# A four-layer graph kernel: layer 3's masks on GpSimd, hop 2's counts a step later, first rows by SyncE's queue

## The chip, the cores and the metric

The kernel runs on one core of one Trainium2 chip. The metric is the device time of one execution in microseconds (us), as the median of several runs. A profiled execution gives the trace from which all durations below come. Engines carry the profile's names: PE is TensorE (PEld its weight loads), DVE is VectorE, ACT is ScalarE, POOL is GpSimd, SP is SyncE; SPq is SyncE's queue of transfers.

## What is computed

The input is x (3327 nodes, 64 features) and a weighted adjacency matrix adj (3327 x 3327). Four layers follow one another, each a residual step with a layer norm: `x = layernorm(x + layer(x))`. Layer 0 and layer 1 (a hyperbolic attention over all pairs of nodes) are not touched here. Layers 2 and 3 are:

```
# layer 2
for k in range(2):                       # hop 1, hop 2
    agg = adj @ x
    x = tanh(concatenate([agg, x], axis=1) @ W[k])

# layer 3
support = input @ weight
mask = (adj != 0)
rank = cumsum(mask, axis=1)
deg = rank[:, -1:]
k = minimum(deg, 100)
pos = rank - (deg - k)
w = mask * where(pos > 0, 0.5 ** (k - pos), 0)
out = w @ support + bias
```

Layer 3 needs, for each entry of adj that is not zero, the number of such entries that follow it in its row; the weight is a power of one half of that number.

## The kernel before

The adjacency matrix lies transposed in HBM, padded to 3328 x 3328 floats: 26 blocks jb of 128 rows (`adjT[jb]`, 1.70 MB each). A block is a tile of 128 partitions x 3328 elements; its two halves h of 1664 columns are worked on apart, and a half holds four chunks of 416 columns. Seven blocks stay in SBUF through layer 2 (`kept`: blocks 19 to 25); the others are loaded anew for each hop.

**Order of work.** From layer 1 on, TensorE's, ScalarE's, VectorE's and GpSimd's instructions stand in the order in which the program writes them (`manual_schedule`). Each engine, and SyncE's queue of transfers, works its own list in that order and waits for semaphores; a buffer that is written anew waits for its last reader.

**Hop 2 of layer 2** (the loop at L585, k = 1) goes through `order`: five blocks still in SBUF from hop 1 (`ready`, so r = 5), then four pairs of a new block and a kept block of the `soon` list (25, 24, 23, 22), then the other new blocks; the last three kept blocks (`end`) come in `chunk_end`. For each block `add` (L514) issues 16 products with `hw`, four for each chunk; a new block is loaded (L216) into one of five buffers, which comes free when the products and the mask of its last block are through.

Beside these products, hop 2 makes masks (1 where adj is not zero, in bf16) and counts them, for layer 3 needs the totals by block before it begins:

- `t_masks` (L444) makes the two half masks of a streamed block into scratch tiles `t_at`; in hop 2 these are the two halves of `tm`.
- `both_masks` (L353) makes the mask of a whole block that is to stay for layer 3. It goes to `over` or to a half of a kept block's tile that hop 2 has used up (`slots_of`); `place` says at which step which block goes where.
- `t_counts` (L451) issues eight products with `upto` for each mask made, which add up the totals by block in PSUM (`t_ps`).

In hop 2 the counts come at once after the masks when both halves of `tm` are made, or when more than four half masks are waiting. When all 26 blocks are counted, `t_out` (L461, L463) writes the totals to HBM (`t_rows`), and `rows_of` (L431) puts each resident block's row of totals into row 0 of its mask, both by GpSimd's queue.

**Layer 3** has 52 steps (h, jb), 26 for each half of the columns; nine blocks' masks are resident, so 34 half masks have to be made anew. `load` (L345) brings a half block into one of four `ah` buffers by SyncE's queue. `masks` (L366) makes its mask on VectorE into one of six buffers of `l3m`, then issues on SyncE's queue the transfer of row 0 (L368) and the next `load`. One of the six buffers is at first `m0`, the first row's entries.

For a step q, `count` (L644) multiplies the mask with a triangular matrix into PSUM bank c (c = 0, 1: two chunks each), `read` turns a bank into weights by a maximum with zero (on VectorE, L657, or on ScalarE, L659), and `products` (L861, and L878 for the low part, gathered over seven steps) multiplies the weights with the features. There is one PSUM tile for each bank, so the next count of a bank waits for its read. In the loop (L1031) step q does, in this order: read bank 0 (ScalarE), read bank 1 (VectorE at odd q, ScalarE at even q), one piece of the list `with_step`, at most one `masks`, and then for each bank the products of step q - 3 and the count of step q + 1.

Before the loop stands the layer's beginning: the last chunks of hop 2 (`chunk_end`), the layer norm of layer 2 (`finish`, `squares`, `sums`, `roots`, `factor`, in four parts A, B, C, E of the blocks) and the splitting of the features into bf16 parts (`first_part`, `rest_of`, `other_parts`). `roots` (L750 to L760) is nine small VectorE operations one after another. What is left of the parts C and E is in `with_step`, and so is `firsts_weighted` (L478 to L480 on VectorE: the weights of the first row of each block, after which `m0` is given back), in the fourth place, and `first_rows` (L893, L897: 16 small transfers by GpSimd's queue of the first rows' features to `sf`), in the seventh. `first_products` (L904) uses both, at step 25 of the loop and once more in the second half.

Of the kernel before, what the change touches and what calls it, by code (L numbers as in the profile page):

```python
# [15 lines left out]
ALU = mybir.AluOpType  # L16
# [5 lines left out]
NB = 26  # L22
NP = NB * P
D = 64
CW = 416
HALF = NP // 2
NBH = NB // 2
# [7 lines left out]
CPH = HALF // CW  # L35
# [10 lines left out]
BATCH_T = 2  # L46
MASKS = 6
# [34 lines left out]
def kernel(  # L82
# [11 lines left out]
    nc = tc.nc  # L94
# [218 lines left out]
    def layers(ctx, x2, x3, begun_here, kept, ready, ahead_ctx, strm):  # L313
# [9 lines left out]
        over = carry.tile([P, NP], BF16, name="over")  # L323
# [12 lines left out]
        mask, ws = {}, {}  # L336

        ahead, to_load = {}, []

        def load():  # L340
            if to_load:
                q = to_load.pop(0)
                h, jb = steps[q]
                ahead[q] = l3w.tile([P, HALF], F32, tag="ah", bufs=LOADS, name=f"ah_{h}_{jb}")
                nc.sync.dma_start(  # L345
                    ahead[q], adjT[jb * P : (jb + 1) * P, h * HALF : (h + 1) * HALF]
                )
# [3 lines left out]
        def both_masks(jb, at):  # L351

            nc.vector.tensor_scalar(at, blocks[jb], 0.0, None, ALU.not_equal)  # L353
            resident[jb] = at
            if jb not in t_done:
                t_done.add(jb)
                t_made.extend((jb, h, m) for h, m in enumerate(halves_of(at)))

        def slots_of(jb):
            at = kept[jb].bitcast(BF16)  # L360
            return at[:, :NP], at[:, NP:]

        def masks(q):
            h, jb = steps[q]
            mask[q] = l3m.tile([P, HALF], BF16, tag="mask", name=f"mask_{h}_{jb}")
            nc.vector.tensor_scalar(mask[q], ahead.pop(q), 0.0, None, ALU.not_equal)  # L366
            half = slice(h * HALF, (h + 1) * HALF)
            nc.sync.dma_start(mask[q][:1, :], t_rows[jb + 1 : jb + 2, half])  # L368
            load()
# [63 lines left out]
        def halves_of(t):  # L433
            return [t[:, h * HALF : (h + 1) * HALF] for h in range(2)]
# [12 lines left out]
        def t_counts():  # L447
            while t_made:
                jb, h, m = t_made.pop(0)
                for c in range(CPH):  # L450
                    nc.tensor.matmul(  # L451
                        t_ps[h][c * 32 : (c + 1) * 32, :], upto[:, 31 - jb : 63 - jb],
                        m[:, c * CW : (c + 1) * CW], start=(h, c) not in t_begun,
                        stop=len(t_done) == NB, skip_group_check=True,
                    )
                    t_begun.add((h, c))
# [25 lines left out]
        with tc.tile_pool(  # L482
# [6 lines left out]
            for k in range(2):  # L489
# [37 lines left out]
                if k:  # L527
                    end = [jb for jb in kept if jb not in soon]
                    r = len(order)
                    for jb in soon:  # L530
                        order += [others.pop(0), jb]
                    order += others
                    place = {
                        1: [(soon[0], over)],
                        r + 1: list(zip(soon[1:3], slots_of(soon[0]))),
                        r + 3: list(zip((soon[3], end[0]), slots_of(soon[1]))),
                        r + 7: list(zip(end[1:], slots_of(soon[3]))),
                    }
                    for i, at in zip((-2, -1), slots_of(soon[2])):
                        place[len(order) + i] = [(order[i], at)]  # L540
                    t_at = halves_of(tm)
                else:
                    stay = list(kept)
                    stay, end = stay[:-2], stay[-2:]
                    share = -(-len(others) // len(stay))
                    for i, jb in enumerate(stay):
                        order += [jb] + others[i * share : (i + 1) * share]
# [38 lines left out]
                for i, jb in enumerate(order):  # L586
                    if jb not in blocks:
                        if len(seen) % (UNDER_WAY + MORE) < MORE :
                            blocks[jb] = held[jb] = block(more, jb, tag="bt", name=f"bt_l2_{k}_{jb}")
                        else:  # L590
                            blocks[jb] = block(strm, jb, tag="at", name=f"at_l2_{k}_{jb}")
                        seen[jb] = blocks[jb]
                    if i or not k:
                        for c in range(CPH):
                            add(c, jb)
                    if k and len(t_made) > 2 * BATCH_T:
                        t_counts()
                    if jb not in t_done and jb not in kept and (k or i >= FIRST_T):
                        t_masks(jb)
                        if len(t_made) >= len(t_at):  # L600
                            t_counts()
                    if k:
                        for b, at in place.get(i, ()):
                            both_masks(b, at)
                    if k == 0 and begun_here:

                        if i == 8:
                            for c in range(CPH):
                                bottom(c)

                            warm_t = small.tile([P, 1], F32, tag="warm", name="warm_t")
                            nc.scalar.activation(warm_t, hT[:, :1], AF.Tanh)
                    if k and len(t_done) == NB and not t_ends:
                        t_ends.append(i)
                        t_counts()
                        t_out()
                        rows_of(resident)
                if k:
# [89 lines left out]
        nc.gpsimd.memset(sf, 0.0)  # L708
        for _ in range(LOADS):
            load()  # L710
        y_all, e_all, p_all = (l3n.tile([P, NB], F32, name=f"root_{k}") for k in "yep")
        parts = ((10, 3), (7, 3), (4, 3), (0, 4))
        A, B, C, E = range(4)
# [62 lines left out]
        def x3_later(i):  # L776
            scaled(i, halves(x3[:, slots(i)]), x3)
# [4 lines left out]
        def first_part(i):  # L782
            nc.scalar.copy(s12[:, slots(i), 0, :], rr[:, slots(i)])

        def rest_of(i):
            sl = slots(i)
            nc.vector.tensor_tensor(rr[:, sl], rr[:, sl], s12[:, sl, 0, :], ALU.subtract)  # L787

        def other_parts(i):
            sl = slots(i)  # L790
            nc.scalar.copy(s12[:, sl, 1, :], rr[:, sl])
            nc.gpsimd.tensor_tensor(s3[:, sl], rr[:, sl], s12[:, sl, 1, :], ALU.subtract)
# [92 lines left out]

        def first_rows():

            with nc.allow_non_contiguous_dma(reason="one row of each block"):
                for cg in range(CPH):
                    e = cg % 2  # L890
                    for h in range(2):
                        at = slice(cg * 32 + h * NBH, cg * 32 + (h + 1) * NBH)
                        nc.gpsimd.dma_start(  # L893
                            sf[at, 0, :],
                            s12[:1, h::2].rearrange("p n t d -> p n (t d)"),
                        )
                        nc.gpsimd.dma_start(sf[at, 1, e * D : (e + 1) * D], s3[:1, h::2])  # L897

        def first_products(h):

# [116 lines left out]
        def firsts_weighted():  # L1017
            nonlocal m0
            first_weights(m0)
            m0 = None  # L1020
# [1 line left out]
        first_out = None  # L1022
        with_step = [
            lambda: other_parts(B), lambda: first_part(C), lambda: rest_of(C),
            lambda: (other_parts(C), firsts_weighted()), lambda: first_part(E), lambda: rest_of(E),
            lambda: (other_parts(E), first_rows()), lambda: x3_later(C), lambda: x3_later(E),
        ]
        products(0, 0)
        advance(1, 2)
        products(0, 1)  # L1030
        for q in range(LEAD, len(steps) + LEAD + 1):  # L1031
            turn = q == NB + LEAD
            read(0, q, False)
            if turn:
                first_out = half_out(0, sums_out(0))
            read(1, q, q % 2 == 1)
            if with_step:
                with_step.pop(0)()
            while consumed and consumed[0] <= q:
                consumed.pop(0)  # L1040
            if to_mask and len(consumed) - len(to_mask) + (m0 is not None) < MASKS:
                masks(to_mask.pop(0))
            p = q - LEAD if q < NB + LEAD else q - LEAD - 1
            for c in range(2):
                if p and not turn:
                    products(p, c)
                if q < len(steps):
                    advance(c, q)
                if turn:
                    next(first_out)  # L1050
            if first_out is not None and not turn:
                next(first_out, None)
# [994 lines left out]
```

## Time and profile before

| what | value |
|---|---|
| runs | 552.70, 553.89, 554.96 us; median 553.89 |
| profiled execution | 552.03 us, of which its span 550.2 |
| busy share | PE 93%, DVE 71%, ACT 53%, POOL 42% |
| layer 3's masks (L366, DVE) | 34, each about 1.02 us |
| hop 2 of layer 2 | about 320 to 405 us |
| beginning of layer 3 | about 405 to 427 us |
| loop of layer 3 | about 427 to 537 us |

A page of the profile has six parts. The first gives busy times by engine, the second 40 equal slices of the span, in tenths; the slices from the 24th on are hop 2 and layer 3:

```profile
PE   8889999999999999999999999888998789989992
DVE  6899999999999999799444231637137986666314
POOL 4599999999999998000000000000260280000000
DMA  8978766666766545799998019957963799975001
```

GpSimd is idle from the 17th slice on but for the transfers and the few small operations at the beginning of layer 3. The fourth part follows the chain that ended last back from the end:

```profile
DMA ah<-in_adjT 4%; PE cnt L644 4%; PE cnt L514 3%; PE acc L861 3%; PE acc L878 3%; DVE w L657 2%; DMA at_l<-in_adjT 2%; DVE mask L366 1%; PE both L732 1%; ACT w L659 1%; PE cnt L923 0%; DVE sq L765 0%; DVE tm L444 0%; DVE l_var L744 0%; DVE sq L787 0%
```

In a timeline a line gives the start and the length in us, the engine, the line of the program, the operation, what it writes and reads with their sizes, and in brackets the idle time of the engine before it with what ended it.

### The profile page before, as it was taken

What the parts mean: (1) busy time and instruction counts of PE and PEld (TensorE: products, weight loads), DVE (VectorE), ACT (ScalarE), POOL (GpSimd) and SP (SyncE); (2) the same over time, 40 slices, a digit from 0 to 9 for tenths busy, and PEclk for the clock granted to TensorE, in tenths of its full rate; (3) what the DMA queues carried; (4) which work ended last, traced back from release to release, by engine and by line L of the source; (5) the groups of instructions that cost most, each with busy time, mean ns of one, the idle gap of its engine ahead of it and who ended that gap; (6) DMA issues with size and microseconds to landing.
All of it is one profiled execution on the core that took longest, in us unless ns stands there. A gap on an engine that the chain in (4) does not pass through costs nothing. (4 is left out here: it accounts for less than half of the span.)

```text
span 550.2 us, 7634 instructions
## 1 busy us (share of the span) xinstructions
PE 509.8 (93%) x2865; PEld 210.8 (38%) x2865; DVE 390.7 (71%) x563; ACT 293.3 (53%) x345; POOL 232.6 (42%) x121
## 2 busy tenths in 40 slices
PE   8889999999999999999999999888998789989992
PEld 5522222222222222854433354333444344454542
DVE  6899999999999999799444231637137986666314
ACT  4899999999999997610000000000016755566641
POOL 4599999999999998000000000000260280000000
PEclk9999999999999999899999999989999999999996
DMA  8978766666766545799998019957963799975001
GB/s 287 366 227 293 244 222 224 240 215 220 238 215 233 184 147 226 299 418 427 424 424 368 0 31 408 412 186 269 414 209 102 259 372 395 404 291 188 0 1 37
DMA packets 34137, 139.20 MB, mean 253 GB/s; under 512 B 11199, under 2 KB 12977, under 8 KB 28971
## 3 DMA queue, kind: packets, MB, share of 16 engines
q1 hardware_dynamic: 30571, 137.40, 67.3%
q0 software_dynamic: 1184, 0.63, 0.5%
q10 hardware_dynamic: 2336, 0.59, 0.5%
q8 instruction: 24, 0.39, 0.3%
q14 instruction: 22, 0.18, 0.1%
HBM read 136.93 MB, written 1.04 MB: 251 GB/s over the span
## 5 line engine op out<-in xcount | busy, mean ns | idle before, releaser
L1260 POOL TENSOR_TENSOR sg<-sg,at 128x1664 f32<-128x1664 f32 x44 | 163.6, 3738 | 1.3 <-ACT sg L1248 1.2
L1288 ACT ACTIVATE pq<-pq,al,ga 128x832 f32<-128x832 f32 x104 | 104.7, 1011 | 10.8 <-DVE a L1287 10.5
L1275 PE MATMUL pq<-riT,ljT 64*128 64x416 f32 x416 | 100.8, 561 | 10.4 <-DVE v L1296 6.2
L1296 DVE SCALAR_TENSOR_TENSOR v<-pq,a 128x832 f32<-128x832 f32 x104 | 105.8, 1018 | 3.2 <-ACT pq L1288 2.2
L1287 DVE SCALAR_TENSOR_TENSOR a<-pq,sg 128x832 f32<-128x832 f32 x104 | 105.7, 1016 | 0.5 <-PE prep_fours L1366 0.4
L1305 PE MATMUL acc<-v,xv 128*64 128x416 f32 x416 | 95.3, 537 | 0.0
L514 PE MATMUL cnt<-at_l,lj 128*64 128x416 f32 x496 | 90.1, 514 | 0.1
L1248 ACT ACTIVATE sg<-lb,rb 128x1664 f32<-128x1664 f32 (+1 forms) x53 | 87.2, 1649 | 0.0
L623 ACT ACTIVATE x<-cnt 128x416 f32<-128x416 f32 x8 | 4.1, 517 | 151.2 <-PE cnt L514 151.2
L659 ACT ACTIVATE w<-cnt 128x832 int16<-128x832 f32 x79 | 65.6, 864 | 34.9 <-PE cnt L644 34.4
L463 POOL DMA_DIRECT2D t_rows<-tb x4 | 2.6, 711 | 148.7 <-DVE tb L461 148.6
L1275 PEld LDWEIGHTS pq<-riT,ljT 64*128 64x128 f32 x416 | 31.3, 184 | 83.7 <-DVE v L1296 82.9
L514 PEld LDWEIGHTS cnt<-at_l,lj 128*64 128x64 f32 x496 | 34.9, 137 | 50.6 <-issue 49.3
L861 PE MATMUL acc<-w,s 128*128 128x416 bf16 x208 | 52.5, 339 | 1.3 <-DVE sq L765 0.5
L1305 PEld LDWEIGHTS acc<-v,xv 128*64 128x64 f32 x416 | 20.6, 134 | 61.8 <-issue 58.0
L657 DVE TENSOR_SCALAR w<-cnt 128x832 int16<-128x832 f32 x25 | 25.5, 1022 | 25.6 <-PE cnt L644 25.6
L514 PE MATMUL cnt<-kept,lj 128*64 128x416 f32 x224 | 43.4, 533 | 0.0
L366 DVE TENSOR_SCALAR mask<-ah 128x1664 bf16<-128x1664 f32 x34 | 35.5, 1058 | 7.0 <-DMA ah<-in_adjT 5.1
L644 PE MATMUL cnt<-mask,tri 128*128 128x416 bf16 x136 | 34.8, 338 | 6.0 <-DVE w L657 3.5
L444 DVE TENSOR_SCALAR tm<-at_l 128x1664 bf16<-128x1664 f32 x20 | 19.5, 1022 | 21.1 <-PE t L451 21.1
L644 PEld LDWEIGHTS <-tri 128*128 128x128 bf16 x208 | 19.5, 97 | 34.4 <-issue 17.7
L1260 POOL TENSOR_TENSOR sg<-sg,kept 128x1664 f32<-128x1664 f32 (+1 forms) x10 | 30.0, 3017 | 0.0
(316 smaller groups left out, 455.5 us busy)
## 6 DMA issues: line engine op xcount, KB each, us to landing
at_l<-in_adjT SPq DMA_DIRECT2D x27, 1664.0 KB, 11.7
at<-in_adjT SPq DMA_DIRECT2D x44, 832.0 KB, 4.8
ah<-in_adjT SPq DMA_DIRECT2D x34, 832.0 KB, 6.4
kept<-in_adjT SPq DMA_DIRECT2D x7, 1664.0 KB
bt_l<-in_adjT SPq DMA_DIRECT2D x6, 1664.0 KB
lb<-lf_rows SPq DMA_DIRECT2D x2, 384.0 KB, 5.7
mask<-t_rows SPq DMA_DIRECT2D x34, 3.2 KB
ljT<-ljT SPq DMA_DIRECT2D x4, 128.0 KB, 3.9
```

The lines of the kernel that those rows point to most:

```text
L366: nc.vector.tensor_scalar(mask[q], ahead.pop(q), 0.0, None, ALU.not_equal)
L514: nc.tensor.matmul(acc[c][h * D : (h + 1) * D, :], hw[:, slot(jb), :], blocks[jb][:, o : o + CW], start=c not in begun, stop=last, skip_gr ...
L644: nc.tensor.matmul(cnt[c][:, e, :], tri, mask[q][:, of], start=True, stop=True, skip_group_check=True,)
L659: nc.scalar.activation(w.bitcast(I16), cnt[c], AF.Relu)
L861: nc.tensor.matmul(acc[h, c][:, e, :], s12[:, slot(jb)].rearrange("p t d -> p (t d)"), ws[q, c][:, e, :], start=first, stop=last,)
L1248: nc.scalar.activation(sg[:, :, of], lbs[:, :, of], AF.Sigmoid, bias=rb[:, sl : sl + 1])
L1260: nc.gpsimd.tensor_tensor(sg[:, :, of], sg[:, :, of], at[:, :, of], ALU.mult)
L1275: nc.tensor.matmul(pq[:, h, :], ljT[h != jb // NBH][rows, of], riT[rows, ch * CW : (ch + 1) * CW], start=True, stop=True,)
L1287: stt(a_s[t], pqs[t], CUBIC_PLUS, us.pop(t), op0=ALU.add, op1=ALU.mult)
L1288: nc.scalar.activation(pqs[t], pqs[t], AF.Square, bias=al[:, one], scale=ga[:, one])
L1296: stt(w, pqs.pop(t), CUBIC_REST, a_s.pop(t), op0=ALU.add, op1=ALU.mult)
L1305: nc.tensor.matmul(accs[cp, ci][h * D : (h + 1) * D, :], xv[:, slot(jb), :], w[:, h, :], start=(jb == orders[cp][0]), stop=(jb == orders[c ...
```

## The change

Four things are done.

1. In hop 2, `place` puts at most one kept mask at a step, and later: the masks stand at steps 1, r+2, r+4, r+5, r+8, r+9 and r+12. From step r+1 on the scratch masks have a second place: the halves of block 25's first slot, in turn with `tm`. `t_counts` is called at each step, after the step's products and before its masks, so masks are counted a step after they were made.
2. `masks` runs on GpSimd, as two comparisons: equal to zero, then less than one half. The first five are issued before the layer's beginning, right after the first loads. Bank 1 is read by VectorE at every step.
3. `firsts_weighted` moves to the tenth place of `with_step` (step 12 of the loop, before step 6).
4. `first_rows` goes to SyncE's queue, two transfers at each of the eight steps 13 to 20.

```diff
         def masks(q):
             h, jb = steps[q]
             mask[q] = l3m.tile([P, HALF], BF16, tag="mask", name=f"mask_{h}_{jb}")
-            nc.vector.tensor_scalar(mask[q], ahead.pop(q), 0.0, None, ALU.not_equal)
+            nc.gpsimd.tensor_scalar(mask[q], ahead.pop(q), 0.0, 0.5, ALU.is_equal, ALU.is_lt)
...
+                    in_first, in_second, in_last = (slots_of(soon[i]) for i in (0, 1, 3))
                     place = {
-                        1: [(soon[0], over)],
-                        r + 1: list(zip(soon[1:3], slots_of(soon[0]))),
-                        r + 3: list(zip((soon[3], end[0]), slots_of(soon[1]))),
-                        r + 7: list(zip(end[1:], slots_of(soon[3]))),
+                        1: (soon[0], over),
+                        r + 2: (soon[1], in_first[1]),
+                        r + 4: (soon[3], in_second[0]),
+                        r + 5: (end[0], in_second[1]),
+                        r + 8: (end[1], in_last[0]),
+                        r + 9: (end[2], in_last[1]),
+                        r + 12: (soon[2], in_first[0]),
                     }
                     for i, at in zip((-2, -1), slots_of(soon[2])):
-                        place[len(order) + i] = [(order[i], at)]
+                        place[len(order) + i] = (order[i], at)
...
-                    if k and len(t_made) > 2 * BATCH_T:
+                    if k:
                         t_counts()
+                    if k and i == r + 1:
+                        t_at = halves_of(in_first[0]) + t_at
                     if jb not in t_done and jb not in kept and (k or i >= FIRST_T):
                         t_masks(jb)
-                        if len(t_made) >= len(t_at):
+                        if k == 0 and len(t_made) == len(t_at):
                             t_counts()
-                    if k:
-                        for b, at in place.get(i, ()):
-                            both_masks(b, at)
+                    if k and i in place:
+                        both_masks(*place[i])
...
-                    if k and len(t_done) == NB and not t_ends:
+                    if k and len(t_done) == NB and not t_made and not t_ends:
                         t_ends.append(i)
-                        t_counts()
                         t_out()
                         rows_of(resident)
...
         for _ in range(LOADS):
             load()
+        for _ in range(MASKS - 1):
+            masks(to_mask.pop(0))
...
-            with nc.allow_non_contiguous_dma(reason="one row of each block"):
-                for cg in range(CPH):
-                    e = cg % 2
-                    for h in range(2):
-                        at = slice(cg * 32 + h * NBH, cg * 32 + (h + 1) * NBH)
-                        nc.gpsimd.dma_start(
-                            sf[at, 0, :],
-                            s12[:1, h::2].rearrange("p n t d -> p n (t d)"),
-                        )
-                        nc.gpsimd.dma_start(sf[at, 1, e * D : (e + 1) * D], s3[:1, h::2])
+            for cg in range(CPH):
+                e = cg % 2
+                for h in range(2):
+                    at = slice(cg * 32 + h * NBH, cg * 32 + (h + 1) * NBH)
+                    yield lambda at=at, h=h, e=e: (
+                        nc.sync.dma_start(
+                            sf[at, 0, :], s12[:1, h::2].rearrange("p n t d -> p n (t d)")
+                        ),
+                        nc.sync.dma_start(sf[at, 1, e * D : (e + 1) * D], s3[:1, h::2]),
+                    )
...
         with_step = [
             lambda: other_parts(B), lambda: first_part(C), lambda: rest_of(C),
-            lambda: (other_parts(C), firsts_weighted()), lambda: first_part(E), lambda: rest_of(E),
-            lambda: (other_parts(E), first_rows()), lambda: x3_later(C), lambda: x3_later(E),
+            lambda: other_parts(C), lambda: first_part(E), lambda: rest_of(E),
+            lambda: other_parts(E), lambda: x3_later(C), lambda: x3_later(E), firsts_weighted,
+            *first_rows(),
         ]
...
-            read(1, q, q % 2 == 1)
+            read(1, q, True)
```

## The prediction

> **What bounds the kernel now.** I read the table of 40 slices first, then the chain of waits, then the timelines of TensorE, SyncE's queue, VectorE and GpSimd for three places that the edits touch: hop 2 of layer 2 (328 to 405 us), the beginning of layer 3 (405 to 427) and its loop (427 to 537). Times are us of the profiled execution: span 550.2, whole 552.03, so 1.83 lie outside the span.
>
> Hop 2 first. TensorE, its timeline:
>
> ```profile
> 345.76 2.96 PE L514 MATMUL cnt<-at_l,lj 128*64 128x416 f32 x16
> 348.65 0.54 PE L451 MATMUL t<-kept,upto 128*32 128x416 bf16 x8
> 349.71 0.54 PE L451 MATMUL t<-kept,upto 128*32 128x416 bf16 x8 [0.52 <-DVE kept L353]
> 350.65 0.36 PE L451 MATMUL t<-tm,upto 128*32 128x416 bf16 x4 [0.40 <-DVE tm L444]
> 351.58 0.36 PE L451 MATMUL t<-tm,upto 128*32 128x416 bf16 x4 [0.57 <-DVE tm L444]
> 351.87 3.01 PE L514 MATMUL cnt<-kept,lj 128*64 128x416 f32 x16
> ```
>
> Here TensorE asks for the counts (L451) of masks that VectorE is still making, and stalls 1.49 us. It does so three times (the timeline has the same triple at 358.66 and 375.51): 4.5 us. The stall also holds a block's buffer, and SyncE's queue waits for that:
>
> ```profile
> 342.21 0.33 SPq L216 DMA_DIRECT2D bt_l<-in_adjT  x1
> 351.59 26.13 SPq L216 DMA_DIRECT2D at_l<-in_adjT  x4
> 380.73 0.33 SPq L216 DMA_DIRECT2D bt_l<-in_adjT  x1
> 384.14 6.53 SPq L216 DMA_DIRECT2D at_l<-in_adjT  x3
> ```
>
> Four loads take 26.13 us to be issued; the windows put the DMA share at 0.77 in 352 to 366 and 0.55 in 366 to 382. Then five loads of 1.70 MB are left at 410 GB/s (4.16 us each), and the last is late: in the chain of waits it is the piece `DMA at_l<-in_adjT` of 11.23 us that starts at 390.34 and lands at 401.57. Both costs together: 22 blocks at 2.85 (64 products in 11.39 us, 16 to a block) and 14 blocks' counts at about 0.44 would end at 327.98 + 62.7 + 6.2 = 396.9; the last block's products ended at 404.46.
>
> The beginning of layer 3 is VectorE's. In the chain of waits:
>
> ```profile
> 411.46 0.18 DVE l_var L750
> 413.38 0.56 DVE sq L765
> ...
> 415.37 0.46 DVE sq L787
> 415.95 0.18 DVE root_y L751
> ```
>
> The chain runs through VectorE from 410.87 to 418.97 almost without a break, in dozens of operations of 0.17 to 0.59 us. Most of these read two tensors of SBUF, or one with SBUF as target.
>
> The loop is paced by the turn of one PSUM bank: counts (L644), reading them (L657 by VectorE, L659 by ScalarE), the next counts into the same bank. Every second pair of L644 is bank 1; these are three in a row, with the read between the first two:
>
> ```profile
> 506.11 0.51 PE L644 MATMUL cnt<-mask,tri 128*128 128x416 bf16 x2
> ...
> 506.73 1.02 DVE L657 TENSOR_SCALAR w<-cnt 128x832 int16<-128x832 f32 x1 [0.51 <-PE cnt L644]
> ...
> 507.81 0.51 PE L644 MATMUL cnt<-kept,tri 128*128 128x416 bf16 x2
> ...
> 509.27 0.51 PE L644 MATMUL cnt<-mask,tri 128*128 128x416 bf16 x2
> ```
>
> A step whose bank 1 is read by VectorE takes 507.81 - 506.11 = 1.70; the next, read by ScalarE, 1.46. Steps with the 28 products of L878 take 4.1 either way. From the fourth count of bank 1 (425.36) to the last (530.16) the loop takes 104.8 for 48 steps.
>
> [...]
>
> ```profile
> 432.17 0.58 DVE L478 TENSOR_SCALAR m<-m 128x832 f32<-128x832 f32 x1
> 432.79 1.02 DVE L479 SCALAR_TENSOR_TENSOR m<-tb,m 128x832 f32<-128x832 bf16 x1
> 433.02 1.57 POOL L792 TENSOR_TENSOR s<-sq,s 128x384 bf16<-128x384 f32 x1 [4.31 <-ACT s L791]
> 433.85 1.19 DVE L480 TENSOR_SCALAR tb<-m 128x832 int16<-128x832 f32 x1
> ```
>
> GpSimd's operation starts at 433.02, waits for L479 (two SBUF inputs) until 433.81 and ends at 434.59; L480, which should take L478's 0.58, takes 1.19 since it is held until then. [...] L1296, from PSUM, keeps 1018 ns beside GpSimd's products L1260. [...] no run here shows a large one-input operation.
>
> **The change, part by part.**
>
> *Hop 2's masks and counts.* Scratch masks get kept block 25's slot beside tm, and their counts stand one block's products (2.85) after they are made; VectorE needs 1.95 for a scratch pair and 1.9 for a kept block, so a pair and a kept block (3.85) lie under two blocks' products (5.7). The three stalls go (-4.5). Buffers are then free when TensorE is through with a block, 2.86 apart or up to 6.6 with a kept block between; the last load is issued near 382 instead of 390.34 and lands near 389, before TensorE wants it at 394. The DMA piece goes too, and TensorE's own work is next: 396.9 against 404.46, -7.6. One stretch ran at a clock of 0.88 (352 to 366, 1.7 us); some of that may stay. I take **-7.0**; bounds -8 and -4 (only the stalls).
>
> *34 masks from VectorE to GpSimd.* VectorE loses 34 x 1.02 us, of which up to 7 us stood in the way of reads in the loop. GpSimd's price is not in the trace. [...] from above L1260's 3.74. The edit compares twice, so I take 1.7. GpSimd then owes 34 x 1.7 = 58 us in 125: it isn't the bound. Each mask still issues its row and the next load on SyncE's queue, in the order of before.
>
> *Five of them before the layer's beginning.* They queue behind GpSimd's row transfers and memsets (405.0 to 408.8 before, near 404 after) and behind the first loads, issued as hop 2 ends (404.67 before, 397 after). Four run back to back, 404 to 411, just where VectorE's chain, 7 us earlier, does its first roots. [...] four masks x 1.7 = 6.8 us in which VectorE gets a few operations of 0.18 in, then a fifth near 412. Nothing covers this, the chain is here. I take **+6.5**. Bounds: 0, if VectorE's small operations slip between [...], and +12 at 2.7 us a mask. The gain, loads that start at once instead of at 428, is hidden: the loop needs 34 loads x 2.08 = 71 us of 105.
>
> *Bank 1 always read by VectorE.* 38 plain steps at 1.70, 6 with L878 at 4.13, the step with the first rows' products at 2.4, three around the turn of the half 9.45, and 1.8 more where the sqrt table is loaded: 103.1 against 104.8, **-1.7**. The stalls behind masks go, but every second step gives back 0.24.
>
> *The first row's weights at step 12 instead of 6.* Three operations, 0.58 + 1.02 + 0.58 less overlaps = 2.1, in a gap of 0.68 between two reads: **+1.4** on the path; before, theirs lay in the 2.34 us stall at 436.96, already in the 104.8. One of six mask buffers is held longer; five masks of lead remain.
>
> *What still contends in the loop.* GpSimd runs one mask per buffer freed, so after nearly each count. rest_of(E), two x3_later, the three weights and the turn's normalisation read SBUF: I count 0.5 for each of the first three, 1.2 for the weights and 1.3 for the turn: **+4.0**, bounds 0 and +8.
>
> *First rows by SyncE.* GpSimd loses 16 issues (11.1 us, 440.8 to 453.2). SyncE gets two of some 0.25 in each of eight steps beside 0.58 for a mask's row and load: 1.1 of 1.7. They land in about 5.5 us (the page's median by GpSimd's queue); the last goes out at step 20, wanted at 25, 8.5 us later. Nothing on the path; if that cover of 3 us went, L904 would wait as long.
>
> Sum: -7.0 + 6.5 - 1.7 + 1.4 + 4.0 = +3.2, 555.2 for the profiled execution. That one is 1.9 under the median of 553.89, so **557.0** as a median.
>
> **Rivals.** *The lock hardly costs (not slower).* VectorE's operations of a few elements slip between masks, or the masks start in its gaps. Price: 1.0 at the beginning instead of 6.5 and 1.0 in the loop instead of 4.0: -7.0 + 1.0 - 1.7 + 1.4 + 1.0 = -5.3, 548.6. It decides if contention costs under 4.5 in all. For it: no small operation meets GpSimd in this trace. Against it: three meetings of larger ones (here, and at 426.92 and 440.23, where L366 takes 1.7 and 1.52 instead of 1.02), all waited for in full. *GpSimd's mask is slow*, 2.6 us [...]: 9.5 at the beginning, 7.5 in the loop, +9.7, 563.6; GpSimd would owe 88 us. *The change to hop 2 doesn't do what it says*: some other wait, say the landing of a block, keeps 6 of the 7: 563.
>
> **How the numbers follow.** Chances: forecast 0.42, light lock 0.32, slow mask 0.16, hop 2 unchanged 0.10. A measurement of this kernel tells about 0.5% (2.8 us) from no change. Faster than 551.1: the light lock and a rest, 0.33; slower than 556.7: half of the forecast's case and the last two, 0.47; between, 0.20. The forecast's own range is 552 to 561; the range of 8 in 10 reaches 546.5 (light lock with a hop-2 gain of 8) and 566 (slow mask and somewhat more).
>
> **What would show it.** Hop 2: no L451 wait on L444 or L353, the last L514 of a streamed block near 397. Beginning: VectorE's root operations stretched from 0.18 to over 1 us beside L366 on GpSimd; if they stay at 0.18, the light lock holds. GpSimd's L366 row: 1.7 or 2.6 us. Loop: bank 1's counts 1.70 apart in plain steps. I am wrong if the beginning, from the last streamed product to the fourth count of bank 1 (20.9 us now), doesn't grow by some 6 us.

## The result and the profile after

The changed kernel takes 649.4 us (median; 648.3 to 651.7) against 553.3 for the kernel before: a ratio of 1.174, 95% interval 1.169 to 1.178. The profiled execution took 648.31, its span 646.4, so the span grew by 96.2. In the code after, line numbers from about 620 on are a few higher: L644 is L648, L657 is L661, L750 to L760 are L756 to L766, L792 is L798, L893 and L897 are L899 and L902, L904 is L910. L366, L451 and L514 keep theirs.

The 40 slices of the page (the span is longer, so layer 3 begins near the 25th), and the first row of its groups (line, engine, operation, tiles, count | busy us, mean ns | idle before it):

```profile
PE   8799999999999999999999999328754477738683
POOL 3799999999999400000000008972999999999930
DMA  8987676666745499996069896640344444445101
```

```profile
L366 POOL TENSOR_SCALAR mask<-ah 128x1664 bf16<-128x1664 f32 x34 | 197.1, 5822 | 0.4 <-PE cnt L648 0.3
```

One mask takes 5.8 us on GpSimd, and GpSimd, which was nearly idle in layer 3, is now the engine that is full, from the 29th slice to the 38th, while PE's digits there lie between 3 and 8 and the DMA digits between 3 and 5 until the loads end. Its timeline says it more sharply, with 27 masks in one piece without a gap:

```profile
402.27 29.09 POOL L366 TENSOR_SCALAR mask<-ah 128x1664 bf16<-128x1664 f32 x5
...
445.35 0.91 POOL L798 TENSOR_TENSOR s<-sq,s 128x384 bf16<-128x384 f32 x1 [13.11 <-ACT s L797]
...
451.01 11.56 POOL L366 TENSOR_SCALAR mask<-ah 128x1664 bf16<-128x1664 f32 x2 [0.35 <-PE cnt L648]
...
463.88 156.43 POOL L366 TENSOR_SCALAR mask<-ah 128x1664 bf16<-128x1664 f32 x27
```

156.43 / 27 = 5.79 each. Between the fifth mask and the sixth GpSimd is idle for some 17 us; the experiment without early masks comes back to this. TensorE's waits from 443 us to the end of the span (waiter, what it waited for: us, times, longest) show who pays:

```profile
PE cnt L648 <- DMA mask<-t_rows: 45.3, 20, 4.6
```

Row 0 of each mask is sent right after the mask, so this wait is named after the transfer (0.25 us on the queue) but is a wait for GpSimd. The loop grows by more than that. From the fourth count of bank 1 to the last, TensorE's waits add up to 62.6 us after and 9.3 before; its busy time is 120.5 us after and 94.9 before, at a mean granted clock of 0.79 and 1.00. GpSimd is busy for 171.1 of the loop's 183.4 us.

Hop 2 in TensorE's timeline, the same place as in the prediction:

```profile
345.40 0.54 PE L451 MATMUL t<-tm,upto 128*32 128x416 bf16 x8
345.86 3.01 PE L514 MATMUL cnt<-at_l,lj 128*64 128x416 f32 x16
348.71 2.96 PE L514 MATMUL cnt<-kept,lj 128*64 128x416 f32 x16
351.60 0.89 PE L451 MATMUL t<-kept,upto 128*32 128x416 bf16 x16
```

No count is followed by a bracket: TensorE waits for no mask any more. On SyncE's queue the four loads that took 26.13 us to be issued take 20.23, and the last three, issued from 384.14 on before, are issued from 375.41 on:

```profile
348.94 20.23 SPq L216 DMA_DIRECT2D at_l<-in_adjT  x4
```

The beginning of layer 3 on VectorE, where an operation of six elements a partition took 0.17 to 0.18:

```profile
403.95 4.26 DVE L756 TENSOR_SCALAR l_var<-l_var 128x6 f32<-128x6 f32 x1
408.24 5.75 DVE L757 TENSOR_SCALAR root_y<-l_var 128x6 int32<-128x6 int32 x1
414.02 4.10 DVE L760 TENSOR_TENSOR root_e<-l_var,root_y 128x6 f32<-128x6 f32 x1
418.16 0.17 DVE L761 TENSOR_TENSOR root_e<-root_e,root_y 128x6 f32<-128x6 f32 x1
```

Each of the first three runs into a mask on GpSimd and is held. The first two end at 408.21 and 413.99, just after the second and the third mask start (408.17 and 413.94), 5.78 apart: one mask. The third ends at 418.12, 1.6 before its mask does (419.73): L761 and the five behind it slip through at 0.17 each beside that mask, and the next that meets one (L731 at 419.89) takes 4.42 instead of 0.59. Such a wait beside an operation of the other engine is what the prediction and the expectations call the lock. The traces show how long it lasts, here twice to a mask's end and twice not, and not what makes it.

VectorE's reads of the counts from PSUM are not held: L661 takes 1022 ns on the average, as L657 did before.

So the span is read in three stretches, cut where the products after the last streamed block's begin and at the fourth and last counts of bank 1:

| stretch | before | after | difference |
|---|---|---|---|
| to the last streamed product | 404.46 | 396.95 | -7.5 |
| beginning of layer 3 | 20.9 | 46.35 | +25.4 |
| loop, 48 steps | 104.8 | 183.4 | +78.6 |

Together +96.5, against 96.2 measured; what follows the last count is 0.35 us shorter.

### The profile page after: what moved, and what is told of

It is laid out like the page before. It is cut to its first block, busy times and chain, and to the rows that moved or that the text cites. A ratio compares the mean times of both kernels' runs of the same rounds, so it can differ in the third digit from the quotient of the medians.

```text
span 646.4 us, 7667 instructions
## 1 busy us (share of the span) xinstructions
PE 536.8 (83%) x2865; PEld 219.5 (34%) x2865; DVE 426.8 (66%) x553; ACT 275.4 (43%) x321; POOL 416.3 (64%) x139
## 4 chain that ended last, share of the span: by engine, by line
PE 48%; POOL 21%; DVE 13%; ACT 8%; issue 6%; DMA 2%; POOLq 1%; DVEq 0%; SPq 0%; ACTq 0%
PE cnt L514 22%; POOL mask L366 20%; PE pq L1282 9%; PE acc L1312 6%; DVE v L1303 4%; ACT pq L1295 4%; ACT sg L1255 3%; PE t L451 2%; DVE l_var L756 2%; DVE a L1294 1%; DVE root_y L757 1%; PE acc L867 1%; PE cnt L505 1%; POOLq L2050 1%; PE both L738 1%
## 5 line engine op out<-in xcount | busy, mean ns | idle before, releaser
L366 POOL TENSOR_SCALAR mask<-ah 128x1664 bf16<-128x1664 f32 x34 | 197.1, 5822 | 0.4 <-PE cnt L648 0.3
L661 DVE TENSOR_SCALAR w<-cnt 128x832 int16<-128x832 f32 x49 | 50.1, 1022 | 98.8 <-PE cnt L648 98.6
L463 POOL DMA_DIRECT2D t_rows<-tb x4 | 4.1, 1050 | 150.0 <-DVE tb L461 150.0
L663 ACT ACTIVATE w<-cnt 128x832 int16<-128x832 f32 x55 | 47.1, 863 | 122.4 <-PE cnt L648 122.3
L514 PE MATMUL cnt<-at_l,lj 128*64 128x416 f32 x496 | 90.5, 515 | 0.0
L648 PE MATMUL cnt<-mask,tri 128*128 128x416 bf16 x136 | 43.4, 408 | 49.0 <-DMA mask<-t_rows 45.3
L867 PE MATMUL acc<-w,s 128*128 128x416 bf16 x208 | 64.1, 401 | 0.6 <-ACT xc L786 0.3
L648 PEld LDWEIGHTS <-tri 128*128 128x128 bf16 x208 | 20.9, 110 | 97.3 <-issue 90.0
L514 PEld LDWEIGHTS cnt<-at_l,lj 128*64 128x64 f32 x496 | 34.4, 137 | 49.8 <-issue 49.4
L514 PE MATMUL cnt<-kept,lj 128*64 128x416 f32 x224 | 41.6, 514 | 0.0
L867 PEld LDWEIGHTS <-s 128*128 128x128 bf16 x208 | 22.7, 112 | 24.9 <-issue 13.7
L648 PE MATMUL cnt<-kept,tri 128*128 128x416 bf16 x64 | 19.0, 389 | 13.5 <-DVE w L661 8.3
```

The source lines that it names most:

```text
L366: nc.gpsimd.tensor_scalar(mask[q], ahead.pop(q), 0.0, 0.5, ALU.is_equal, ALU.is_lt)
L514: nc.tensor.matmul(acc[c][h * D : (h + 1) * D, :], hw[:, slot(jb), :], blocks[jb][:, o : o + CW], start=c not in begun, stop=last, skip_gr ...
L648: nc.tensor.matmul(cnt[c][:, e, :], tri, mask[q][:, of], start=True, stop=True, skip_group_check=True,)
L661: nc.vector.tensor_scalar(w.bitcast(I16), cnt[c], 0.0, None, ALU.max)
L867: nc.tensor.matmul(acc[h, c][:, e, :], s12[:, slot(jb)].rearrange("p t d -> p (t d)"), ws[q, c][:, e, :], start=first, stop=last,)
```

## The experiments

Two theories stood against each other. The first: the loss is the price of GpSimd's operation, which makes GpSimd the bound, and the other parts are about what the prediction said. The second: the loss is contention, in the beginning or with moved transfers, and a cheaper operation alone wouldn't mend it. Times are medians; "before" was measured beside each, and its medians lay between 554.25 and 554.75.

**The forms by themselves**, three operations of each on one 128 x 1664 tile, alone but for one operation of VectorE at the start:

```diff
+    for _ in range(TIMES):
+        g.tensor_scalar(o16, a, 0.0, 0.5, ALU.is_equal, ALU.is_lt)
...
+    for _ in range(TIMES):
+        g.tensor_scalar(o16, a, 100.0, 1.0, ALU.mult, ALU.add)
...
```

> Only GpSimd operations on one 128 x 1664 tile, three of each form, with nothing beside them; all four layers are left out. First theory (the comparisons are dear): two comparisons take 5.8 us here too, alone, and half of that less the fixed part at 832 elements; one comparison takes about 2.9, and multiply, minimum and copy take 1.6 to 2. Rival one (the change of type is dear): every form that goes from f32 to bf16 takes about 5.8, whatever it computes, and the forms f32 to f32 and bf16 to bf16 take 1.6 to 3. Rival two (the 5.8 us are contention with VectorE or with transfers): all forms take 1.6 to 2 here.

One line of the timeline, with the kernel's own form (L35: two comparisons, f32 to bf16), then groups by line (busy us, mean ns): L39 is two comparisons from f32 to f32, L45 one comparison, L47 a multiplication alone, L51 multiply and add.

```profile
17.79 5.79 POOL L35 TENSOR_SCALAR o<-a 128x1664 bf16<-128x1664 f32 x1
...
L39 POOL TENSOR_SCALAR o<-a 128x1664 f32<-128x1664 f32 x3 | 17.4, 5792 | 0.0
...
L47 POOL TENSOR_SCALAR o<-a 128x1664 bf16<-128x1664 f32 x3 | 13.2, 4405 | 0.2
L45 POOL TENSOR_SCALAR o<-a 128x1664 bf16<-128x1664 f32 x3 | 13.2, 4401 | 0.2
...
L51 POOL TENSOR_SCALAR o<-a 128x1664 bf16<-128x1664 f32 x3 | 4.7, 1577 | 0.2
```

5.79 us with nothing beside it: not contention. (The first of the three L35 took 6.65; VectorE's one large operation waits for the same load.) Not the types either: two comparisons take 5.80 from bf16 to bf16 and 5.79 from f32 to f32. And not the comparisons as such, as I had expected: a multiplication alone takes as long as a comparison alone, and multiply and minimum 5.80. A copy takes 1.57, multiply-add 1.58. At 832 elements two comparisons take 2.99, so by these two sizes 0.18 is fixed and an element costs 3.37 ns (an estimate).

**More forms**, to find which are quick:

```diff
+        g.tensor_scalar(o16, a, 1.0, 2.0, ALU.add, ALU.add)
...
+        g.tensor_scalar(o16, a, 2.0, 3.0, ALU.mult, ALU.mult)
...
+        g.tensor_scalar(o16, a, 0.5, 0.2, ALU.min, ALU.max)
...
```

> More of GpSimd's forms by themselves on a 128 x 1664 tile, all four layers left out. Theory one [...]: only multiply-add takes 1.58, with a 16-bit integer as target too; all others 4.4 or 5.8. Theory two (additions and multiplications are quick in any order, comparisons, minimum and maximum are slow): add-multiply, add-add and multiply-multiply take 1.58 as well. The same forms at 832 elements take half less a fixed part of some 0.2. Two inputs: 2.96 to 3.74, by the type of the target.

Neither theory holds. Quick (1.57 to 1.58): multiply-add, also with a 16-bit integer as target, add-multiply, multiply-multiply and minimum-maximum. Slow pairs (5.81): add-add, subtract-multiply, comparison-multiply. A lone addition takes 4.41. So four pairs (and a copy) are quick and everything else that was tried with one input is not; what sets them apart stays open. One line of it was of use: minimum-maximum is quick, and can make a mask.

**The hop 2 edit alone**: the kernel before with the diff's hunks on `place`, `t_at`, `t_counts` and `t_ends`, nothing else.

```diff
-                    if k and len(t_made) > 2 * BATCH_T:
+                    if k:
                         t_counts()
+                    if k and i == r + 1:
+                        t_at = halves_of(in_first[0]) + t_at
...
```

> The kernel before with the new order of hop 2's masks and counts and nothing else of the change. Theory: the 7.5 us that the trace of the changed kernel shows at the last streamed product are kept to the end, about 546. Rival: layer 3 gives them back, since its loads and GpSimd's row transfers aren't 7.5 earlier, 550 to 553.

546.8 (545.8 to 548.7), a ratio of 0.986 (0.983 to 0.989): 7.8 us less. With one later version at 547.0 it is the fastest here; no version with layer 3's masks on GpSimd came below 552.5.

**Hop 2 put back** in the changed kernel, the same hunks the other way round:

```diff
-                    if k:
+                    if k and len(t_made) > 2 * BATCH_T:
                         t_counts()
...
```

> The changed kernel with hop 2's masks and counts put back as before. Theory (the loop waits for GpSimd's 34 masks, so what hop 2 gives is carried to the end in full): 649 plus 6 to 8, 655 to 658. Rival (hop 2's gain is hidden where GpSimd is the bound): 648 to 651.

657.05, which is 7.65 more than the changed kernel. Hop 2 gives nearly the same with slow masks on GpSimd as it did by itself.

**No masks before the layer's beginning**, on GpSimd with two comparisons still:

```diff
-        for _ in range(MASKS - 1):
-            masks(to_mask.pop(0))
```

> The changed kernel without the five masks before the layer's beginning: all 34 are issued in the loop, on GpSimd. Theory (GpSimd's time for 34 masks, 197 us, sets the end): the beginning loses its 25 us, but the masks start some 15 to 20 us later and the end hardly moves, 640 to 652. Rival (the lock at the beginning is a loss of its own): 25 less, about 624.

650.25 against 649.4. The beginning shrank from 46.35 to 20.85 and the loop grew from 183.4 to 208.6 by the same 25. The stretching of the beginning is real, but taking the early masks away gains nothing. Counted from the start of hop 2 (at 326.6 and 329.3 us in the two traces), GpSimd's first mask starts after 75.7 us in the changed kernel and after 94.3 in this one, but its last mask ends after 293.7 and 293.3. So the early start is worth nothing, since GpSimd is idle for 17 us after its fifth mask: of the six buffers five hold masks and one holds `m0`, and what comes next in its list (L798, then the sixth mask, which waits for a count) needs the beginning that the five masks stretched. What five early masks would give if they held nothing up, these two runs don't show.

**One comparison for two**, which leaves ones and zeros as they are:

```diff
-            nc.gpsimd.tensor_scalar(mask[q], ahead.pop(q), 0.0, 0.5, ALU.is_equal, ALU.is_lt)
+            nc.gpsimd.tensor_scalar(mask[q], ahead.pop(q), 0.0, None, ALU.is_gt)
```

> The changed kernel with one comparison (greater than 0) in place of two; it gives the same ones and zeros. By itself this form took 4.40 us against 5.79. Theory (GpSimd's 34 masks set the end, each 1.39 cheaper): 649 less 47, about 602. Rival (masks aren't what the loop waits for): the same as the changed kernel.

604.7: 44.7 less, where 34 x 1.39 = 47.3 was expected. The time follows the operation's price nearly one to one. Carried on in a straight line, these two runs meet the kernel before at a mask of about 2.9 us (an estimate: 44.7 us for 1.37 us a mask in the two traces, and 50 more to go from 4.45).

**The price that the prediction took.** The same line with multiply by 1 and add 0:

```diff
-            nc.gpsimd.tensor_scalar(mask[q], ahead.pop(q), 0.0, 0.5, ALU.is_equal, ALU.is_lt)
+            nc.gpsimd.tensor_scalar(mask[q], ahead.pop(q), 1.0, 0.0, ALU.mult, ALU.add)
```

> The changed kernel with one line altered: GpSimd's mask operation multiplies by 1 and adds 0, the form that took 1.58 us by itself. The tile so made holds adj's values in place of ones, so the counts of 34 half blocks are not the reference's; all else stands. This is the price that the prediction assumed (1.7). Theory (only this price was wrong): what the prediction's sum gives, 553 to 560 (forecast 557). Rival one (the lock is light at such a length): 546 to 551. Rival two (first rows by SyncE's queue cost as well, since two of its issues take 1.6 us and not 0.5, so loads and rows of masks come late): 3 to 6 over the forecast, 558 to 563.

552.6 (549.2 to 555.8), a ratio of 0.996 (0.994 to 0.998). 97 us are gone with one line, and at the assumed price the whole change is 2 us quicker than the kernel before. That is just under the 553 to 560 of the theory and above the 551 of the light lock: the price explains the loss, and the rest of the prediction's sum was some 4 us too dear for this run. VectorE's beginning in this run:

```profile
410.56 1.55 DVE L756 TENSOR_SCALAR l_var<-l_var 128x6 f32<-128x6 f32 x1
412.14 0.17 DVE L757 TENSOR_SCALAR root_y<-l_var 128x6 int32<-128x6 int32 x1
...
412.55 1.51 DVE L761 TENSOR_TENSOR root_e<-root_e,root_y 128x6 f32<-128x6 f32 x1
```

The same picture with shorter masks: an operation of 0.17 is held for up to 1.6 us, a few slip through, and the next is held. The beginning takes 28.0 here, 7.1 more than before.

**The same in the reference's computation.** GpSimd clamps adj (zero or at least 0.05) to 2^-20; TensorE's triangular matrix for these masks is 2^20 times as large, its first row (the totals) excepted.

```diff
+QUICK = 2.0**-20
...
+    tri_q = const.tile([P, P], BF16, name="tri_q")
+    nc.vector.tensor_scalar(tri_q, tri, 1.0 / QUICK, None, ALU.mult)
+    nc.vector.memset(tri_q[:1, :], -STEP)
...
-            nc.gpsimd.tensor_scalar(mask[q], ahead.pop(q), 0.0, 0.5, ALU.is_equal, ALU.is_lt)
+            nc.gpsimd.tensor_scalar(mask[q], ahead.pop(q), QUICK, 0.0, ALU.min, ALU.max)
...
-                    cnt[c][:, e, :], tri, mask[q][:, of], start=True, stop=True,
+                    cnt[c][:, e, :], tri if steps[q][1] in resident else tri_q,
+                    mask[q][:, of], start=True, stop=True,
```

> The changed kernel with GpSimd's masks made by a minimum with 2^-20 and a maximum with 0 (adj is zero or at least 0.05, so the mask holds 0 or 2^-20), and a second triangular matrix, 2^20 times the first but for its first row, for these masks; the computation is the reference's. A pair minimum, maximum took 1.57 us by itself. Theory (the price of the operation is all): 551 to 554, as with multiply and add. Rival (true masks behave otherwise than adj's values did, or the form is slow at these constants): over 560.

554.5, a ratio of 1.001 (0.999 to 1.004): no change against before, just above what I had expected. It settles the cause: the same masks but for their scale, by the same engine in the same places, in a form of 1.6 us, and 95 of the 96 us are not lost.

**Fewer masks ahead**, in that version: none, then two.

```diff
-        for _ in range(MASKS - 1):
+        for _ in range(2):
```

> The run with minimum and maximum, without the five masks before the layer's beginning. If those five cost what the beginning shows (7 us) and nothing is lost by starting later: 545 to 548. If the masks then start too late for the loop, which waits for them: 550 to 556.

> The run with minimum and maximum, with two masks before the layer's beginning instead of five; these two run at 403 to 408, where they meet one or two of VectorE's operations. Theory (each mask that meets VectorE's chain costs its length once): the beginning grows by 1.5 to 3 instead of 7, 547 to 550. Rival (a start with three masks fewer is paid back in the loop): 551 to 555.

None: 554.05 (ratio 0.998 to 1.003); two: 552.5 (0.996 to 0.999). Both fell where the rivals said. The stretches of the three profiles:

| masks ahead | beginning | loop | both |
|---|---|---|---|
| 0 | 20.8 | 111.9 | 132.7 |
| 2 | 22.8 | 106.8 | 129.6 |
| 5 | 26.3 | 103.9 | 130.2 |

What the early masks cost in the beginning they give back in the loop; without them TensorE waits 3.6 us there for late masks' rows, with two or five for none. Between none and five no difference is left. Two ahead are 2.0 us quicker than five, and their intervals don't touch, so the last three of the five cost a little more than they give.

**Only the rest of the change**, with masks on VectorE again, in the loop only, and bank 1 in turn:

```diff
-            nc.gpsimd.tensor_scalar(mask[q], ahead.pop(q), 0.0, 0.5, ALU.is_equal, ALU.is_lt)
+            nc.vector.tensor_scalar(mask[q], ahead.pop(q), 0.0, None, ALU.not_equal)
...
-        for _ in range(MASKS - 1):
-            masks(to_mask.pop(0))
...
-            read(1, q, True)
+            read(1, q, q % 2 == 1)
```

and in the second of these runs, besides `first_rows` by GpSimd's queue as before,

```diff
-            lambda: other_parts(E), lambda: x3_later(C), lambda: x3_later(E), firsts_weighted,
-            *first_rows(),
+            lambda: (other_parts(E), first_rows()), lambda: x3_later(C), lambda: x3_later(E), firsts_weighted,
```

> The changed kernel with the masks on VectorE in the loop as before (so none before the layer's beginning) and bank 1 read by both engines in turn; hop 2, the later weights of the first rows and the first rows by SyncE's queue stay. Theory (all of the loss is GpSimd's masks): 544 to 548, within 2 of the hop 2 edit alone. Rival (the moved first rows and weights cost, too): over 549.

> The hop 2 edit, masks on VectorE in the loop, first rows by GpSimd's queue as before; of the rest only the later weights of the first row (step 12) stay. Against 546.8 for the hop 2 edit alone and 551.8 with the first rows on SyncE's queue too. If SyncE's issues are the cause of those 5 us: 546 to 548.5. If the later weights are: 550 to 553.

The first, with first rows on SyncE's queue, took 551.8 (ratio 0.991 to 0.998), the second, with them on GpSimd's queue and only the weights later, 547.0 (0.983 to 0.989). So my theory that all of the loss is GpSimd's masks was wrong by the rows: on SyncE's queue they cost some 4.8 us when masks are made on VectorE. The later weights cost nothing (546.8 without them). SyncE's queue in the first of the two runs (L897 and L900 are the rows):

```profile
453.57 0.79 SPq L897 DMA_DIRECT2D sf<-s  x1
454.41 0.75 SPq L900 DMA_DIRECT2D sf<-s  x1
455.28 0.35 SPq L368 DMA_DIRECT2D mask<-t_rows  x1
456.99 0.35 SPq L345 DMA_DIRECT2D ah<-in_adjT  x1
```

A row's two issues take 1.54, and with 0.7 for the mask's row and the load the queue owes 2.24 in a step of 1.6 to 1.7. In that run TensorE waited 7.3 us for masks' rows; in the second 1.5.

**First rows back on GpSimd's queue, with quick masks there** (the last diff again, on the run with multiply and add):

> As the run with multiply and add, but the first rows' 16 transfers stand in GpSimd's queue and at the step where they stood before the change. Against that run: if SyncE's queue is what is late, 3 to 6 us less; if it isn't (GpSimd then loses 8 to 11 us of issues between its masks), the same or up to 5 more.

557.8, 5.2 more than with SyncE's queue (552.6). The 16 issues stand between two masks, and TensorE waits once 5.6 us for a mask. So the better queue depends on who makes the masks: with masks on VectorE it is GpSimd's, by 4.8 us, with quick masks on GpSimd it is SyncE's, by 5.2.

**Quick masks on GpSimd and nothing else of layer 3's changes**, on the hop 2 edit:

```diff
-            nc.vector.tensor_scalar(mask[q], ahead.pop(q), 0.0, None, ALU.not_equal)
+            nc.gpsimd.tensor_scalar(mask[q], ahead.pop(q), 1.0, 0.0, ALU.mult, ALU.add)
```

> The kernel with the hop 2 edit alone (546.8), and of the rest only that the masks in the loop are made by GpSimd in the form that takes 1.58 us, so 34 tiles hold adj's values in place of ones; nothing before the layer's beginning, bank 1 read in turn, first rows as before. Theory (VectorE's masks stood before reads in the loop, a quick mask elsewhere frees up to 5 us): 541 to 546. Rival [...]: 547 to 552.

556.9, 10 above the hop 2 edit alone: slower still than the rival's range, and only in part because VectorE's operations are held beside masks: its three weights take 1.96, 1.61 and 1.85, 2.6 more than in the hop 2 edit's trace. The loop's wait for a mask behind the 16 issues (5.2 us in one piece) is the largest wait, which neither theory had. How the rest divides wasn't taken apart.

**Bank 1 in turn, with quick masks:**

```diff
-            read(1, q, True)
+            read(1, q, q % 2 == 1)
```

> The run with multiply and add in GpSimd's masks (552.6, tiles with adj's values in place of ones), with bank 1 read by VectorE and ScalarE in turn, as before the change. The prediction gave bank 1 on VectorE alone 1.7 us of gain. If that holds: 553.5 to 555. If reading in turn is the quicker way (1.58 a step on the average against the 1.63 to 1.70 of VectorE alone, once no mask stands before VectorE's reads): 548 to 551.

552.6, ratio 0.993 to 0.997, against 0.994 to 0.998: no difference that can be told, and between the two ranges.

Five early masks on VectorE were not tried.

## Why the prediction was wrong

The step that failed is the price: "from above L1260's 3.74. The edit compares twice, so I take 1.7. GpSimd then owes 34 x 1.7 = 58 us in 125: it isn't the bound." The mask takes 5.79, above that upper end; GpSimd owes 34 x 5.79 = 197 us, and it is the bound. The upper bound was no bound: L1260 has two inputs and takes 3.74 for 1664 elements (3738 ns a piece in the page of before), and the prediction assumed that an operation with one input can't be dearer. The 1.7 was my estimate, which no run had shown. The quick forms come near it (1.58 us, and 0.89 at 832 elements, so some 0.83 ns an element), this one doesn't: (5.79 - 0.18) / 1664 is 3.37 ns an element, and a lone comparison, at 4.40, is at 2.5 if as much of it is fixed.

The trace of the kernel before held a hint. A GpSimd operation of 26 elements takes 0.22 there. That is a multiply-add, the form that turned out quick; next to it stand a maximum and multiplication (L1506) and a lone multiplication (L1508) of the same size, which take longer:

```profile
L1506 POOL TENSOR_SCALAR gs<-g 128x26 f32<-128x26 f32 x1 | 0.3, 344 | 0.1
L1508 POOL TENSOR_SCALAR gks<-gk 128x26 f32<-128x26 f32 x1 | 0.3, 304 | 0.1
...
L1510 POOL TENSOR_SCALAR aav<-aa 128x26 f32<-128x26 f32 x1 | 0.2, 223 | 0.1
```

The order is that of the large ones: pair, lone operation, multiply-add. It is a hint and no measure, for other things may have stretched operations so small. The sentence in the prediction that "no run here shows a large one-input operation" was the place to widen the range: the rival of the slow mask stopped at 2.6 us and 88 us owed, short of the 125 of the stage, 3.7 us a mask. Even the bound of 3.74, multiplied out, gave 127; by the estimate from the runs GpSimd decides from about 2.9 us a mask, since it also stands idle between the early masks and the rest.

The other steps:

- *Hop 2*, -7.0: right in size (-7.5 in the trace, -7.8 and -7.65 in the two runs that isolate it), and in mechanism for the stalls, which are gone (4.5 us of TensorE's waits before, none after). The late load, the second cost in its sum, hardly was one: in the trace before TensorE is idle for 0.14 of the 23 us from 382 to 405. Instead, 1.7 us before are one block at a lower clock (4.71 for 3.01 at 360.82, where the granted clock was 0.63 against 1.00 from 354 to 360), which the prediction thought might stay; no trace with the edit has it, nor the one with hop 2 put back. From its start to the last streamed product hop 2 takes 77.75 us before, 76.63 where it is put back and 70.35 with the edit. So the size was met in part by luck.
- *Five before the beginning*, +6.5: right in that VectorE's small operations are held (up to 5.76 us for 0.17 in the changed kernel), though not always to a mask's end. At the price that was meant it measured +7.1 with multiply-add and +5.5 with the clamp (26.3 against 20.8), at the real price +25.4. What failed is the clause that the gain of an early start is hidden: with the clamp five masks ahead shorten the loop by 8.0, and no net loss is left against none (554.5 and 554.05).
- *Bank 1 by VectorE*, -1.7: not borne out. Steps came 1.63 apart, but in turn the mean of 1.70 and 1.46 is 1.58, and the runs show no difference.
- *Weights at step 12*, +1.4: too much; 547.0 against 546.8.
- *What still contends*, +4.0: my estimate, and still open. The sum had 104.8 - 1.7 + 1.4 + 4.0 = 108.5 for the loop. One trace has 107.8 (multiply-add), another 103.9 (the clamp).
- *First rows by SyncE*, 0: the second wrong price. I took 0.25 for an issue, which is that of a mask's row; these took 0.74 to 0.94. On GpSimd's queue the trace before already had 0.50 to 1.38 for each of the same transfers. With VectorE's masks that is 4.8 us. In the changed kernel it hides under GpSimd's 5.8 us a mask (one wait for `sf`, 1.0 us).

With the price put right the forecast of 557.0 would have been 2.5 to 4.4 us above the two runs that test it, which came out even with the kernel before or 2 us quicker. Only the price explains the other 95 us.

What stays open: why some pairs are quick on GpSimd; and why executions spread over some 6 us (549.2 to 555.8 with multiply-add, 551.8 to 558.3 in one series of the kernel before). A part of the spread arises ahead of what was changed: in the traces hop 2 begins between 326.6 and 331.6 us, while its length is 70.35 us in all 13 traces with the edit. A loop's length, from one profile, is good to a few us only.

## What to carry to other kernels

Before work is moved to an engine, measure that exact form of the operation there, by itself: on the same tile one pair of operations took nearly four times as long here as another (5.79 and 1.58 us), and no neighbouring row bounded it. Then write down what the engine owes in the stage and from which price on it would be the bound; idle time that the change itself brings to that engine counts as well. If the unknown price can reach that point, that is the slower case to put into the range. A transfer that is moved to a queue costs the issue time of its own shape, which is read from its own row and not from another transfer's (here 0.74 to 0.94 us against the 0.25 of a mask's row).

## What was not expected of the hardware

- GpSimd's `tensor_scalar` on 128 x 1664: 5.8 us for five of the nine pairs of operations tried, 4.4 for a lone one, 1.57 to 1.58 for multiply-add, add-multiply, multiply-multiply and minimum-maximum. A lone multiplication (4.41) is thus dearer than multiply-add (1.58).
- VectorE's operations of six elements are held while GpSimd's mask runs: up to 5.76 us for 0.17 of work. A few of them slip through: in the changed kernel six in a row at 0.17 each from 418.16 us on, while the third mask runs until 419.73, and with multiply-add seven from 404.91 us on, six of them in the gap from 404.98 to 406.31 between two masks.
- Small strided transfers took 0.74 to 0.94 us each on SyncE's queue, three times the 0.25 of a mask's row there.
- In the changed kernel, where TensorE waits often, its granted clock is lower: 0.68 from 470 to 520 us, with TensorE busy for 26.46 of the 50, against 1.00 from 382 to 397, where it is busy throughout. Pairs of counts in the loop take up to 0.90 instead of 0.51 us. Over the execution the clock is 0.906, against 0.984 for the hop 2 edit alone. That the waits are the cause isn't shown.
